# A graph-attention kernel on one core: part-filled gather columns packed densely at computed lane offsets, and more columns weighted by ScalarE in layer 1

## The chip, the core and the metric

The kernel runs on one core of one Trainium2 chip. The metric is the time of one execution on the device in microseconds (us), as a median over runs. Engines go by the profile's names: PE (TensorE, matrix products), DVE (VectorE), ACT (ScalarE), POOL (GpSimd) and SP (SyncE, whose queue issues plain DMAs). Indirect DMAs, which gather rows at addresses that lie in a tile, are issued by GpSimd.

## What is computed

A graph of 6250 nodes with 256 features and 100000 directed edges (`src`, `dst`, sorted by `dst`) goes through three attention layers. Layers 1 and 2 are GATv2 (4 heads of 64) with an ELU between them; their sum with `x` is normalised. Layer 3 is GAT (8 heads of 32) with a residual and a second normalisation. Cut to what matters:

```python
def _gatv2_layer(x, src, dst, n, Wl, Wr, att, b):       # layers 1 and 2, with a loop at each node
    xl = (x @ Wl).reshape(n, H, C)
    xr = (x @ Wr).reshape(n, H, C)
    e = leaky_relu(xl[src] + xr[dst], 0.2)
    logits = einsum('ehc,hc->eh', e, att)
    alpha = softmax of logits over the edges of each dst
    return segment_sum(xl[src] * alpha[:, :, None], dst, n) + b

def _L1_gnn_ref(h, W, a, src, dst):                     # layer 3
    Wh = einsum('nf,hfd->hnd', h, W)
    e = leaky_relu(s1[:, src] + s2[:, dst], 0.2)        # s1, s2: Wh with the halves of a
    attn = softmax of e over the edges of each dst
    out = segment_sum(attn[:, :, None] * Wh[:, src], dst, N)

x = _layernorm(x + _L0_gnn_ref(x, ...))
x = _layernorm(x + _L1_gnn_ref(x, ...))
```

## The kernel before

**Batches and columns.** `make_plan` sorts the nodes by the number of their incoming edges, most first, and cuts them into 49 batches of 128. A batch has one node on each of 128 partitions, called lanes here. Column j of a batch is the j-th neighbour of every lane: one indirect DMA fetches 128 rows of the layer's table (260, 261 or 264 floats each). Since the nodes are sorted, the number of columns falls from batch to batch. The function `columns` fixes the numbers before the run from the expected spread of degrees, 3.5 standard deviations wide: 27 for batch 0, then 25, 24, 23, 22, 21, 21, ... to 10, 10, 9, together 803. A last column of a batch that only a few lanes can fill need not be gathered alone. Ten such columns (of batches 3, 13, 17, 26, 31, 36, 40, 43, 47 and 48) share 3 packs: a pack is one gather of 128 rows whose lanes belong to several batches at fixed offsets, and `lay_rows` (L1415) copies each batch's lanes into its row tile. `lack_rows` (L1422) fills the lanes that are left with a row that belongs to nobody, so that it gets no weight. That makes 796 gathers a layer.

**Row tiles.** The rows of a batch lie in two to four tiles `g` of up to 9 columns, taken in turn from a pool of 9 (`rowp`, ROWS = 9). In layers 1 and 2 column 0 is the node itself.

**Lists.** `near_r` holds for each batch the nodes' own features and the list of neighbours; `start1` (L1887) fetches a batch's part with one indirect DMA, in layer 1 three batches ahead. After a batch in layer 1 the list is overwritten by the neighbours' places in the sorted order (`spots`, L1822), which address the tables of layers 2 and 3.

**Order.** Everything stands in an order written out by hand, and each engine works its own list from front to back. In layers 1 and 2 (`layer2`), iteration b runs `attend(b)`: for each row tile VectorE makes z = max(g, pr), z times `at`, and a sum per head (L1777 for the first tile, made one batch ahead, L1797, L1800, L1801), then the maximum `top` (L1579), and ScalarE the exponentials (L1587). `weighted_sum` multiplies the rows by their weights: VectorE most columns (L1633), ScalarE the last `few` of a batch, one instruction for each column and head (L1629); PE adds the columns up in `acc` (L1640). `few` is a third of the columns in layer 1 and two thirds in layer 2. `finish` turns the sums into the next layer's table rows, which SP writes (L1917 in layer 1, L1960 in layer 2). At the end of the iteration `fetch(b + 2)` lets GpSimd gather the columns of batch b + 2 (`gather_rows`, L1438). Layer 3 goes the same way with a smaller logit step (L2010) and its sums on VectorE (L1662, L1674); there GpSimd also writes the results out, one indirect DMA a batch (L2040).

**From layer to layer.** The three batches with the most columns have their lists sorted by address (`sort_sources`), so that the first 14, 12 and 11 columns of batches 0, 1 and 2 (`EARLY`) come from table rows of batches 0 to 44. Their gathers (`begin`, with the list `soon`) stand behind the last gather of the layer before. The other gathers of the next layer stand behind them and read the whole table.

**Packs before.** `pick_rows` (L1402) copies the lanes' addresses into a small tile `pick` by plain DMAs from SBUF to SBUF, from layer 1's lists and, for the later layers, from `spots`.

## Time and profile before

| | |
|---|---|
| median of 3 runs | 3244.62 us (3239.51 to 3245.31) |
| profiled execution | 3236.04 us, span 3234.2 us |
| DVE busy | 2714.0 us, 84% of the span, 2609 instructions |
| POOL busy | 2414.4 us, 75%, 2587 instructions |
| PE busy | 1399.5 us, 43% |
| ACT busy | 1281.5 us, 40% |
| moved by DMA | 397.64 MB, 123 GB/s; GpSimd's queue 336.86 MB, the queue of SP and ACT 57.08 MB |
| plan | to about 99 us |
| layer 1 | 1549 gathers from `xl_d` in layers 1 and 2 together, from 102.9 us |
| layer 2 | first `soon` gather at 1157.97 us |
| layer 3 | first `soon` gather at 2155.40 us, last gather at 3214.76 us |

Every duration comes from one profiled execution. In a group's row the columns are busy time and the mean of one instruction, then the idle time of the engine just before them and what ended most of it; "issue" is time in which the engine waited for nothing that the profile shows. In a timeline row they are the start, the duration, the engine and line, what it writes and reads, and in brackets the idle time before it. The profile shortens names: `xl_d` stands for the tables of layers 1 and 2 alike.

### The profile page before, as it was taken

The numbers are of one execution on the slowest core, as the hardware profiler recorded it, in microseconds if no ns is written. First come the engines' busy times: TensorE is split into PE (matmuls) and PEld (weight loads), VectorE is DVE, ScalarE is ACT, GpSimd is POOL, SyncE is SP. The second block draws the span as 40 slices with busy tenths as digits, with TensorE's granted clock in tenths as the row PEclk, the third lists the DMA queues.
The fourth block names the chain that finished last, engine by engine and source line by source line (L and its number), as shares of the span: only waits on it lengthen the run. The fifth ranks groups of instructions, "written<-read, shape, count | busy, mean of one in ns | idle before, by whom it ended". The sixth has DMA issues, their size and how long they took to land.

```text
span 3234.2 us, 25459 instructions
## 1 busy us (share of the span) xinstructions
PE 1399.5 (43%) x5423; PEld 1123.4 (35%) x5424; DVE 2714.0 (84%) x2609; ACT 1281.5 (40%) x5161; POOL 2414.4 (75%) x2587
## 2 busy tenths in 40 slices
PE   8356657666676854666556566760000000000000
PEld 6245545555565643545444455550000000000000
DVE  8599999898899979999989999984966766766777
ACT  4234444444445535777667777770000000000000
POOL 5677777777777777777777777777777777777776
PEclk9678888778888886787788778885555555555555
DMA  9444444444444454444444444444333333333333
GB/s 262 123 113 125 119 120 122 118 122 124 123 123 126 126 146 116 122 123 129 128 123 127 133 129 134 135 129 113 108 107 109 110 108 107 109 109 110 109 110 93
DMA packets 176463, 397.64 MB, mean 123 GB/s; under 512 B 50923, under 2 KB 93955, under 8 KB 176283
## 3 DMA queue, kind: packets, MB, share of 16 engines
q0 software_dynamic: 120608, 336.86, 38.7%
q1 hardware_dynamic: 53992, 57.08, 5.8%
q10 hardware_dynamic: 1700, 1.97, 0.2%
q8 instruction: 48, 0.79, 0.1%
q14 instruction: 115, 0.94, 0.1%
HBM read 354.60 MB, written 40.42 MB: 122 GB/s over the span
## 4 chain that ended last, share of the span: by engine, by line
POOL 25%; DVE 18%; issue 14%; DMA 5%; PE 3%; ACT 0%; DVEq 0%; POOLq 0%; ACTq 0%
POOL g L1438 24%; DVE z L1800 4%; DVE lg L1801 4%; DMA g<-xl_d,near_r 3%; DVE z L1797 3%; PE acc L1640 3%; DVE z L1777 2%; DVE g L1633 2%; DMA g<-whs_d,near_r 1%; DVE weighted L1662 1%; POOL out L2040 1%; DMA out<-y,node_i 1%; DVE stats L1684 0%; DVE acc_v L1674 0%; DVE at L1600 0%
## 5 line engine op out<-in xcount | busy, mean ns | idle before, releaser
L1438 POOL DMA_INDIRECT g<-xl_d,near_r x1549 | 1465.6, 946 | 472.6 <-issue 417.6
L1640 PE MATMUL acc<-g,ident 128*128 128x256 f32 x3408 | 966.5, 452 | 631.3 <-DVE g L1633 318.4
L1640 PEld LDWEIGHTS acc<-g,ident 128*128 128x128 f32 x3408 | 778.4, 232 | 820.4 <-DVE g L1633 336.3
L1438 POOL DMA_INDIRECT g<-whs_d,near_r x756 | 719.5, 952 | 230.3 <-issue 220.5
L1629 ACT ACTIVATE g<-g,by 128x64 f32<-128x64 f32 x3080 | 744.9, 336 | 28.4 <-DVE by L1596 28.4
L1801 DVE TENSOR_REDUCE lg<-z 128x28 f32<-128x1820 f32 (+4 forms) x234 | 497.3, 2125 | 8.1
L1800 DVE TENSOR_TENSOR z<-z,at 128x1820 f32<-128x1820 f32 (+4 forms) x234 | 496.6, 2122 | 4.7
L1797 DVE TENSOR_TENSOR z<-g,pr 128x1820 f32<-128x1820 f32 (+3 forms) x138 | 299.6, 2171 | 42.9 <-DMA g<-xl_d,near_r 33.7
L1604 ACT ACTIVATE wt<-lg 128x128 f32<-128x128 f32 (+17 forms) x49 | 14.0, 285 | 801.5 <-DVE lg L1603 801.5
L1674 DVE TENSOR_REDUCE acc_v<-weighted 128x256 f32<-128x3584 f32 (+10 forms) x47 | 319.0, 6787 | 1.6
L1633 DVE TENSOR_TENSOR g<-g,at 128x256 f32<-128x256 f32 (+8 forms) x185 | 273.5, 1496 | 3.3
L1587 ACT ACTIVATE at<-lg,top 128x19 f32<-128x19 f32 (+14 forms) x392 | 115.3, 294 | 378.2 <-DVE top L1579 359.5
L1777 DVE TENSOR_TENSOR z<-g,pr 128x2080 f32<-128x2080 f32 (+4 forms) x96 | 197.8, 2061 | 72.3 <-DMA g<-xl_d,near_r 33.3
L2010 DVE TENSOR_TENSOR lg<-g,s_r 128x56 f32<-128x56 f32 (+4 forms) x111 | 22.9, 214 | 255.5 <-DMA g<-whs_d,near_r 234.6
L1662 DVE TENSOR_TENSOR weighted<-g,wt 128x1792 f32<-128x1792 f32 (+4 forms) x111 | 227.0, 2056 | 0.3
L1563 ACT COPY xT<-pt 128x256 f32<-128x256 f32 x147 | 50.2, 374 | 403.4 <-PE pt L1558 403.4
L1568 PE MATMUL pm<-wcat,xT 128*128 128x260 f32 x392 | 94.2, 383 | 1.4 <-ACT xT L1563 1.4
L1568 PEld LDWEIGHTS pm<-wcat,xT 128*128 128x128 f32 x392 | 74.2, 190 | 13.3 <-ACT xT L1563 2.1
L1587 ACT ACTIVATION_READ_ACCUMULATOR at<-lg,top 128x1 f32 x392 | 73.2, 187 | 0.0
L1568 PE MATMUL pm<-wh_cat,xT 128*128 128x272 f32 x196 | 58.6, 422 | 22.6 <-ACT xT L1563 22.6
L2040 POOL DMA_INDIRECT out<-y,node_i x49 | 49.8, 1015 | 22.8 <-issue 14.1
L1688 ACT ACTIVATE sd<-mv,eps 128x1 f32<-128x1 f32 x98 | 29.0, 296 | 91.5 <-DVE mv L1686 91.3
(267 smaller groups left out, 1591.5 us busy)
## 6 DMA issues: line engine op xcount, KB each, us to landing
g<-xl_d,near_r POOLq DMA_INDIRECT x1549, 2.8
g<-whs_d,near_r POOLq DMA_INDIRECT x756, 2.8
whs_d<-row SPq DMA_DIRECT2D x49, 132.0 KB
xl_d<-row SPq DMA_DIRECT2D x49, 130.0 KB
xr_d<-row SPq DMA_DIRECT2D x49, 130.0 KB
two<-xl_d SPq DMA_DIRECT2D x49, 130.0 KB
two<-xr_d SPq DMA_DIRECT2D x49, 130.0 KB
near_d<-x_all SPq DMA_DIRECT2D x7, 896.0 KB
```

The costliest lines, as they stand in the source:

```text
L1438: nc.gpsimd.indirect_dma_start(out=g[:, j + own - s0, :width], out_offset=None, in_=table, in_offset=source(of, b, j),)
L1568: nc.tensor.matmul(pm, xT[:, c, :], w[:, c, :], start=c == 0, stop=c == 1)
L1587: nc.scalar.activation(wt[:, :, h], lg[:, :S, h], AF.Exp, bias=top[:, h : h + 1], accum_out=den[:, h : h + 1],)
L1629: nc.scalar.mul(g4[:, t, h, :], g4[:, t, h, :], by[:, s0 + t - a0, h : h + 1])
L1633: nc.vector.tensor_mul(g4[:, :m], g4[:, :m], wt[:, s0 : s0 + m, :].unsqueeze(3).to_broadcast([P, m, H, F // H]),)
L1640: nc.tensor.matmul(acc, ident, g4[:, t], start=False, stop=s0 + t == S - 1 and not more)
L1662: nc.vector.tensor_mul(prod[:, s0 - base : s1 - base, :].rearrange("p t (h d) -> p t h d", h=H), g[:, :n, :F].rearrange("p t (h d) -> p t ...
L1674: nc.vector.reduce_sum(part, prod[:, : s1 - base, :].rearrange("p s f -> p f s"), axis=AX.X)
L1777: nc.vector.tensor_max(z, rows[0][:, :n, :W2], xr[:, None, :].to_broadcast([P, n, W2]))
L1797: nc.vector.tensor_max(z, g[:, :n, :W2], xr[:, None, :].to_broadcast([P, n, W2]))
L1800: nc.vector.tensor_mul(z, z, at[:, None, :].to_broadcast([P, n, W2]))
L1801: nc.vector.reduce_sum(lg[:, s0:s1, :], z.rearrange("p t (h d) -> p t h d", h=H2), axis=AX.X)
```

## The change

The column number of every batch stays; which of the columns are gathered as a whole and which by packs changes.

- `lanes_of` (new, before the run) lists every column that fewer than 96 lanes are sure to fill: 33 items (batch, column), among them two columns of batches 1, 2 and 47 and three of 48. For each it gives the most lanes that it may have (`top`, 8 to 128) and bounds `lo` and `hi` on the sum of lanes of all items before it. The columns that stay are `base`, 770 in all. The items fill 14 packs.
- `find_lanes` (new, once, ahead of layer 1's first gather) computes on the chip how many lanes each item has, sums them up by a product with ones and a scan, brings the sums within `lo` and `hi`, and stores them as integers in `lane_i`. `late` collects whether a bound was broken; then the general path would run as well. It also makes `shut`, which is added to the logits of lanes that an item lacks.
- `pick_lanes` (new, layer 1) writes the addresses of each item into the DRAM list `pick_d` at the item's offset, which SP loads into a register (`lane`). The writes overlap: each covers `top` lanes, and the next one overwrites what the item does not fill. When all items of a pack are written, its 128 addresses are read back into `picks[0]`.
- `gather_packs` gathers pack q behind the dense columns of batch `upon[q]` (1, 1, 1, 3, 5, 7, 8, 15, 19, 20, 25, 34, 44, 46), `keep_packs` writes it to DRAM (`pack_d`), and `lay_rows` reads each item's lanes from there, at the register's offset, into the row tile. For the later layers the packs' own addresses are taken from layer 1's rows (`picked`).
- In layer 1 the lists of the batches whose items are needed are fetched before a batch's gathers: those of batches 3 to 20 ahead of batch 1's, to 25 at batch 3, and so on.
- `weighted_sum` in layer 1 gives ScalarE two fifths of a batch's columns instead of a third, at most all but one of the last tile's.
- The 7 `spare` gathers of `make_plan` and the ten adjustments of `most` go; `counts` moves to a pool that outlives the plan.

```diff
@@ columns / lanes_of
-    packs, taken = [], set()
...
+    for b in range(1, NB):
+        size = min(P, N - P * b)
+        for c in range(low, cols[b]):
+            if min(size, over[c] - 3.5 * sd[c] - P * b) < 0.75 * P:
+                base[b] = min(base[b], c)
+                items.append((b, c))
+                top.append(max(8, min(P, -(-math.ceil(over[c] + 3.5 * sd[c] - P * b) // 8) * 8)))
...
+    K = -(-hi[-1] // P)
+    need = [min(items[i][0] for i in range(len(items)) if hi[i] + top[i] > P * q) for q in range(K)]
+    last = [max(i for i in range(len(items)) if lo[i] < P * (q + 1)) for q in range(K)]
@@ make_plan
-    for k in range(SPARE):
-        nc.gpsimd.indirect_dma_start(
-            out=spare[:, k, :], out_offset=None, in_=listed,
-            in_offset=bass.IndirectOffsetOnAxis(ap=begin_i[:, k : k + 1], axis=1),
-        )
@@ tile_by_degree
+    upon = [max(1, b - 1) for b in need]
...
+    def find_lanes(zp, ps):
...
+        for b, own in items_of.items():
+            nc.vector.tensor_scalar(
+                has[:, own[0] : own[-1] + 1], numbers[:, base[b] : cols[b]], counts[:, b : b + 1],
+                None, op0=OP.is_lt,
+            )
+        pn = ps.tile([P, len(items)], F32, name="lane_n", tag="tp")
+        nc.tensor.matmul(pn, ones, has, start=True, stop=True)
+        nc.vector.tensor_scalar(shut, has, -1.0, BIG, op0=OP.add, op1=OP.mult)
...
+    def lane(i):
+        _, (v,) = nc.values_load_multi_w_load_instructions(
+            lane_i[:, i : i + 1], engines=[mybir.EngineType.SP], min_val=lo[i], max_val=hi[i],
...
+        return bass.ds(v, top[i])
+    def pick_lanes(lists):
+        while written[0] < len(items) and items[written[0]][0] < lists:
+            i = written[0]
+            b, c = items[i]
+            nc.sync.dma_start(pick_d[lane(i), :], sources[: top[i], b, c : c + 1])
+            for q in range(K):
+                if filled_by[q] == i:
+                    nc.sync.dma_start(picks[0][:, q : q + 1], pick_d[q * P : (q + 1) * P, :])
+            written[0] += 1
-        nc.sync.dma_start(rows[-1][:n, rows_at[b], :width], held_rows[q][r : r + n, :width])
+    def keep_packs(b, k):
+        for q in packs_at.get(b, ()):
+            nc.sync.dma_start(pack_d[k][q * P : (q + 1) * P, :], held_rows[q][:, : wide[k]])
+            if k == 0:
+                nc.sync.dma_start(
+                    picked[:, q : q + 1], pack_d[0][q * P : (q + 1) * P, W2 : W2 + 1]
+                )
+    def lay_rows(b, rows, cut, own, k):
+        for i in items_of.get(b, ()):
+            j = items[i][1] + own
+            g, s0 = next((g, s0) for g, (s0, s1) in zip(rows, cut) if s0 <= j < s1)
+            nc.sync.dma_start(g[: top[i], j - s0, : wide[k]], pack_d[k][lane(i), :])
+    def shut_lanes(b, lg, own, H):
+        if b in items_of:
+            i0, n = items_of[b][0], len(items_of[b])
+            s = lg[:, base[b] + own : cols[b] + own, :]
+            nc.vector.tensor_add(s, s, shut[:, i0 : i0 + n].unsqueeze(2).to_broadcast([P, n, H]))
@@ layer2, gather(b)
+                if i == 0 and b:
+                    lists = max([b + 2] + [items[filled_by[q]][0] for q in range(K) if upon[q] <= b]) + 1
+                    for k in range(min(NB, lists)):
+                        begins(k)
+                    pick_lanes(lists)
+                gather_rows(b, rows, cut, 1, table, of, width, first, base[b])
+                gather_packs(b, pack_tile, picks[i], table, width)
+                lack_rows(b, rows, cut, 1, table, width)
+                if b == 1:
+                    waiting.append(lambda: (keep_packs(b, i), lay_rows(b, rows, cut, 1, i)))
+                else:
+                    lay_rows(b, rows, cut, 1, i)
+                    waiting.append(lambda: keep_packs(b, i))
@@ layer2, attend(b)
-                few = min(S // 3, cut[-1][1] - cut[-1][0] - 1) if i == 0 else (2 * S - 2) // 3
+                shut_lanes(b, lg, 1, H2)
+                few = min(2 * S // 5, cut[-1][1] - cut[-1][0] - 1) if i == 0 else (2 * S - 2) // 3
@@ layer2, before gather(0)
+                find_lanes(zp, pst)
+                pick_lanes(3)
@@ layer 3: gather_packs, keep_packs, lay_rows and shut_lanes in the same places
```

## The prediction

> **What bounds the kernel now.** I read the page's busy shares first, then its costliest groups, then busy time by stage, then the timelines of GpSimd and of SP's queue around the two changes of layer.
>
> ```profile
> span 3234.2 us, 25459 instructions
> PE 1399.5 (43%) x5423; PEld 1123.4 (35%) x5424; DVE 2714.0 (84%) x2609; ACT 1281.5 (40%) x5161; POOL 2414.4 (75%) x2587
> ...
> L1438 POOL DMA_INDIRECT g<-xl_d,near_r x1549 | 1465.6, 946 | 472.6 <-issue 417.6
> ```
>
> VectorE is the busier engine by share (2714 against 2414 us), but the share is no verdict. A gather takes GpSimd 0.95 us, and 0.30 us of "issue" follows each one: 1.25 us from start to start. The timeline keeps that step without a hole from 102.9 to 3214.8 us: 64 or 65 DMAs in each 80 us. 2489 indirect DMAs at 1.25 us are 3111 us of the span of 3234.2. So GpSimd's queue sets the pace now, and one DMA fewer is worth 1.25 us, as long as nothing else comes last. What else could, the stages show (columns: us, then PE, PEld, DVE, ACT, POOL busy):
>
> ```profile
> core 0: us, PE busy (x) PEld busy (x) DVE busy (x) ACT busy (x) POOL busy (x), PEclk, DMA share, GB/s
> ...
> 380.10:900.90 520.80, 342.49 (x1336) 280.39 (x1337) 470.34 (x382) 229.65 (x940) 394.09 (x417) 0.81 0.45 121
> 900.90:1178.50 277.60, 210.75 (x834) 171.13 (x833) 263.87 (x256) 143.84 (x592) 209.85 (x223) 0.88 0.49 130
> ...
> 1496.20:1910.50 414.30, 249.93 (x911) 198.40 (x912) 376.30 (x305) 294.38 (x1212) 313.16 (x333) 0.79 0.46 128
> 1910.50:2170.40 259.90, 178.66 (x632) 139.39 (x631) 249.84 (x238) 202.69 (x835) 196.55 (x209) 0.83 0.48 133
> 2249.50:3205.10 955.60, 0.00 (x0) 0.00 (x0) 688.98 (x731) 63.57 (x184) 724.41 (x760) 0.50 0.39 109
> ```
>
> The bounds are starts of the softmax maximum (L1579), which VectorE does once a batch: rows one and two are layer 1's batches 9 to 31 and 32 to 48, three and four the same of layer 2, the last is layer 3. VectorE leaves about 0.03 us between instructions, so its true waiting is 50.5 - 382 x 0.03 = 39 us in row one, 13.7 - 7.7 = 6 in row two, 38.0 - 9.2 = 29 in row three, 10.1 - 7.1 = 3 in row four, and over a quarter of layer 3. In the last third of layers 1 and 2 VectorE has almost nothing left to give. There a faster GpSimd only runs ahead, until it meets this:
>
> ```profile
> 1156.59 0.95 POOL L1438 DMA_INDIRECT g<-xl_d,near_r  x1 [0.30 <-issue]
> 1157.97 0.94 POOL L1438 DMA_INDIRECT g<-xl_d,soon  x1 [0.43 <-PE acc L1640]
> ...
> 1204.59 0.95 POOL L1438 DMA_INDIRECT g<-xl_d,near_r  x1 [0.30 <-issue]
> ```
>
> ```profile
> 1153.62 0.33 SPq L1917 DMA_DIRECT2D xl_d<-row  x1
> ...
> 1194.19 0.32 SPq L1917 DMA_DIRECT2D xl_d<-row  x1
> ```
>
> The `soon` gathers of the next layer read rows of batches 0 to 44, so the first of them waits for batch 44's table row; the first `near_r` gather needs batch 48's. Batch 44's write is issued at 1153.62. What a write takes to land is seen at the end of layer 2:
>
> ```profile
> 2147.60 0.34 SPq L1960 DMA_DIRECT2D whs_d<-row  x1
> ```
>
> ```profile
> 2150.40 0.95 POOL L1438 DMA_INDIRECT g<-xl_d,near_r  x1 [0.30 <-DMA whs_d<-row]
> ...
> 2155.40 0.94 POOL L1438 DMA_INDIRECT g<-whs_d,soon  x1 [0.30 <-PE acc L1640]
> ```
>
> GpSimd is released by that landing at 2150.1, 2.5 us after issue. So at the first change of layer batch 44's row is there at 1156.1 and is used at 1157.97: slack 1.9 us. At the second it is 2155.40 - 2150.1 = 5.3 us. Batch 48's rows (1194.19 and 2185.84 plus 2.5) have 8 and 13 us.
>
> **The change, part by part.** *Gathers.* Before, a layer has 803 columns, 10 of them in 3 packs: 796 gathers. After, 770 dense columns and 14 packs: 784. 12 fewer in each layer, 15 us of GpSimd a layer, 45 in all. But not evenly. In layer 2, GpSimd is ahead of its old place by 2 gathers at batch 8, 3 at 20, 6 at 31, 10 at 46, 12 at 48. In layer 1 the node lists (`start1`, one DMA a batch) needed to fill the packs are fetched early: 18 before batch 1's gathers instead of 4. So GpSimd's data there are *later*: by 12 DMAs at batch 1, 24 (30 us) at 8, 20 at 20, 11 at 26, 3 at 31, none at 36, and ahead by 4 at 40 and 12 at 48.
>
> *Layer 1.* From batch 8 to 30 VectorE waits for gathers already, so it slips with them: 30 us at batch 8, 25 at 20, 14 at 26, some 4.5 at 31. It catches up because its 39 us of waiting are used up. From 31 on it is bound by itself. The shutting add comes to 13 of these batches; small VectorE adds of this size take 0.17 to 0.20 us (L1594, L1491), so 2.6 us. ScalarE takes one more column in 17 of them, 0.27 us each (L1633: 0.94 us for 3 columns, 1.75 for 6): 4.6 us. Of the 6 us of waiting perhaps 4 can close. 4.5 - 4 - 4.6 + 2.6 = -1.5: VectorE ends layer 1 about 1.5 us sooner, and with it batch 44's row. GpSimd, 15 us ahead, stands still before `soon` and gains 1.5 + 1.9 = 3.4 us.
>
> *ScalarE's share.* 28 more columns in the layer, four scalings at 0.24 us from start to start: 1 us a batch, 27 us in all, on an engine that works 40 of 80 us. PE reaches these columns last: 26 matmul instructions of batch 42 run from 1096.05 to 1104.9 and ScalarE's four columns are done at 1099.07, so a fifth at 1100.0 is hidden. Without that cover it would be 1 us a batch, some 20 us.
>
> *Layer 2.* GpSimd's data are 6 x 1.25 = 7.5 us earlier at batch 31, where VectorE still waits for them. After it: 13 adds, +2.6, and 1 us of waiting to close: VectorE ends 7.5 - 2.6 + 1 = 6 us sooner beyond the 3.4. Batch 44's row then allows 6 + 5.3 = 11.3 of the 15 us.
>
> *Layer 3.* VectorE has a quarter free, no table follows, so all 15 us count. At its end the last batch has 6 gathers instead of 9, 8.8 us, and VectorE needs 10.5 us for batch 47 (3205.1 to 3215.6); but the step was 13.2 us before, and the gain stays 15.
>
> *Round trips on SP.* Each lane goes pack, DRAM, row tile: 14 writes and 33 reads a layer, each read after a register load (0.63 to 0.76 us on SP before) and an issue of about 0.5. Packs are gathered a batch or more before their lanes are needed, except for batch 1: packs land about 196 in layer 1, kept by 199, laid by 205. VectorE's batch 1 then ends some 28 us late instead of 17, which vanishes behind the 30 us at batch 8. In layers 2 and 3 the same chain ends at about 1250 and 2248, and VectorE comes to it at 1252.4 and 2249.5: hidden with 2 us to spare; without that cover 2 to 5 us. Behind these waits on SP stand the writes of table rows and the loads of `two`; a batch's SP work adds up to some 10 to 15 us, and the shortest batch has 12.5 to 14. Batch 44's write has about 7 us of room behind the lays of 47.
>
> *Filling the picks (layer 1).* Each write of lanes waits for the one before, since they overlap. Ten writes (items 4 to 13) and one read stand between batch 3's node list (141 us) and the packs of batch 1, at 160.5 + 23 x 1.25 = 189 us. A step is issue plus landing: no row has a chained write of 4-byte elements. Below: 0.5 + 2.5 = 3.0 us by the table row; above, what the view of the tile `moved` says of its only DMA, the writes of 152-byte runs to `near_d` (L1237):
>
> ```profile
> DMA to landing us min/median/max: 5.1/7.5/9.1
> ```
>
> that is 0.5 + 7.5 = 8.0. GpSimd's wait is 141 + 11 x step - 189: none up to 4.4 us, 40 us at 8.0. I take 3.0, since 512 bytes are nearest to one small transfer, `moved` being 171 KB. The Trainium skill ("DMA: Bandwidth & Descriptors", the section on the anatomy of one DMA) puts about 2 us of fixed cost on a DMA, mostly the receipt of the write and heaviest in HBM, and its quick reference says that pieces under 512 B are read, modified and written. By the first a step would be an estimated 2.5 us, the chain hidden and the sum the same; the second speaks against this change, and only a run can price it.
>
> *The rest at nothing.* `find_lanes` is some 120 small VectorE instructions, about 15 us before batch 0; VectorE idles 27 us there, and batch 1 comes 17 us later anyway; uncovered, 15. The 7 `spare` gathers (10 us) and ten small operations go from GpSimd's plan, where it then waits 15.3 us for VectorE (L1237).
>
> **Sum.** 3.4 + 11.3 + 15 = 29.7 us. Against the profiled execution (3236.0 us, span 3234.2) that is 3206; it was 8.6 us below the median of 3244.6, so the median becomes 3215.
>
> **Rivals.** *All of it* (10%): VectorE's ends move with GpSimd, 45 us, 3200. For it: VectorE waits 29 to 39 us in mid-layer. Against: the 6 and 3 us at the ends. *Layer 3 alone* (10%): VectorE absorbs nothing, its adds and stalls on PE (`pr` came within 2 us of being late in half of layer 1's batches) eat the rest, 15 us, 3230. *The pick chain, slower than before* (15%): GpSimd waits in layer 1's batch 1. Up to batch 30 nothing lies idle that could win it back, so it counts nearly whole. It decides from a step of (48 + 30) / 11 = 7.1 us; at 8.0, 10 us slower, 3255. For it: SP's order and the row of `moved`. Against: its bytes. *The lanes don't fit their bounds* (1%) and the whole general path runs as well, far slower; the bounds are 3.5 deviations wide.
>
> **How the numbers follow.** Forecast 64%: 3215, with step between 3 and 5.5 us (12 us of wait) and VectorE's ends off by 8 us either way: 3206 to 3228. Eight in ten reaches to the full gain and half of the chain's stall: 3200 to 3238. A measurement here can tell about 0.2%, 6.5 us. Faster by more: the forecast, both smaller-gain rivals, less a tenth for a stall near 25 us, 0.78. Within: 0.06. Slower: 0.16.
>
> **What would show it.** Right: GpSimd's group of gathers falls by 12 a layer at 946 ns; a wait of about 12 us at the first `soon` gather after layer 1, about 4 after layer 2, none in layer 3; VectorE some 25 to 30 us late near 380 us and level by 1180. Wrong: GpSimd waiting for picks near 190 us; waits for `pack_d` on VectorE; waits of VectorE for `pr` beyond 7 us.

## The result, and the profile after

The changed kernel takes 3278.26 us (median of 4 runs, 3276.50 to 3281.29) where the kernel before takes 3244.1: ratio 1.0109, 95% interval 1.0091 to 1.0126. It is slower by 34 us, five times what a measurement can tell; the forecast was 29 us faster. The profiled execution took 3276.66 us.

The page's span, busy shares and largest group:

```profile
span 3274.9 us, 26659 instructions
...
PE 1407.0 (43%) x5425; PEld 1126.5 (34%) x5426; DVE 2729.3 (83%) x2817; ACT 1307.8 (40%) x5274; POOL 2375.4 (73%) x2533
...
L1536 POOL DMA_INDIRECT g<-xl_d,near_r x1503 | 1425.9, 949 | 472.8 <-issue 414.7
```

GpSimd has 54 instructions fewer, since the gathers went as planned, and it is busy 39 us less. But its waits (engine and line, what for; us in all, times, longest) have new entries:

```profile
POOL two L1493 <- DMA pick<-pick_d: 39.8, 4, 21.8
...
POOL g L1536 <- DVE g L1731: 12.7, 2, 12.4
...
POOL g L1536 <- DVE few_got L1544: 8.5, 1, 8.5
```

The first are the packs of batch 1, in GpSimd's timeline:

```profile
202.58 0.95 POOL L1536 DMA_INDIRECT g<-xl_d,near_r  x1 [0.30 <-issue]
203.83 0.95 POOL L1493 DMA_INDIRECT two<-xl_d,pick  x1 [0.30 <-issue]
226.57 0.95 POOL L1493 DMA_INDIRECT two<-xl_d,pick  x1 [21.78 <-DMA pick<-pick_d]
238.57 0.94 POOL L1493 DMA_INDIRECT two<-xl_d,pick  x1 [11.06 <-DMA pick<-pick_d]
...
1199.63 0.95 POOL L1536 DMA_INDIRECT g<-xl_d,near_r  x1 [0.30 <-issue]
1212.93 0.94 POOL L1536 DMA_INDIRECT g<-xl_d,soon  x1 [12.36 <-DVE g L1731]
```

Pack 0 finds its picks, packs 1 and 2 wait 33 us for theirs, and nothing else on GpSimd can run meanwhile. What they wait for is SP's chain of writes (start, time from the first issue to the end of the last, number; the last four lines are the first packs on their way to DRAM):

```profile
151.15 32.84 SPq L1479 DMA_DIRECT2D pick_d<-near_r  x5
194.68 0.34 SPq L1482 DMA_DIRECT2D pick<-pick_d  x1
195.53 21.64 SPq L1479 DMA_DIRECT2D pick_d<-near_r  x4
223.87 0.34 SPq L1482 DMA_DIRECT2D pick<-pick_d  x1
224.72 2.85 SPq L1479 DMA_DIRECT2D pick_d<-near_r  x2
235.83 0.34 SPq L1482 DMA_DIRECT2D pick<-pick_d  x1
...
236.71 0.35 SPq L1500 DMA_DIRECT2D pack_d<-two  x1
239.03 0.33 SPq L1502 DMA_DIRECT2D picked<-pack_d  x1
239.40 0.43 SPq L1500 DMA_DIRECT2D pack_d<-two  x1
242.55 0.33 SPq L1502 DMA_DIRECT2D picked<-pack_d  x1
```

The chain begins at 125.96. Its 14 writes and what follows each of them until SP goes on come to 68.7 + 28.3 + 11.1 = 108 us: 7.7 us a step. Single steps of 24 to 40 lanes took 2.5 to 7 us, those of 104 to 128 lanes 7 to 11 us; the longest (9 to 11 us) came while row gathers ran or were still landing beside them, but the last, of 128 lanes with GpSimd standing still, took 8.6 as well. A pack's write, 128 pieces of 1 KB, holds up the read that waits for it by 2.3 and 3.2 us only (236.71 to 239.03, 239.40 to 242.55). The picks' reads back, also in 4-byte pieces, are short: the last is issued at 235.83 and the pack starts at 238.57.

The third entry is the start. The view of the tile `pick_d` says who waited for its first fill (L1423, 1,920 pieces of 4 bytes, issued at 100.91):

```profile
L1423 SPq DMA_DIRECT2D pick_d<-nowhere x1: 410/410/410, 100.9 to 100.9; - x1
...
  DVE few_got L1544: 21.8, 1
```

The first node list, issued at 101.38, landed at 112.5, 11 us later; before it took 3 us (99.00 to 101.93). The first row gather starts at 113.47 instead of 102.9. That the fill is what the list waits for is the profile's inference. The kernel without picks, below, drops the fill and keeps the three broadcasts issued right behind it; there the first list landed 3.3 us after its issue (100.07 to 103.40).

VectorE's stages, between the same batches as those shown of before:

```profile
core 0: us, PE busy (x) PEld busy (x) DVE busy (x) ACT busy (x) POOL busy (x), PEclk, DMA share, GB/s
465.49:962.64 497.15, 345.40 (x1342) 282.75 (x1343) 468.73 (x393) 241.32 (x992) 372.81 (x393) 0.82 0.52 123
962.64:1234.36 271.72, 204.97 (x828) 166.71 (x827) 261.73 (x267) 158.19 (x652) 193.58 (x206) 0.90 0.54 129
```

It reaches the first 85 us later than before and the end of the second 56 later. Its waiting in the first fell from 39 us to 497.15 - 468.73 - 393 x 0.03 = 17, in the second from 6 to 2: it used up what it had, and that gave back 26 of the 85; 3 more came from its shorter work (some 2 us less in each stretch). So the stall at batch 1 counts at the end of the layer. Batch 44's table row (the write at 1210.11, landed by 1212.6 with the 2.5 us of the prediction) comes just ahead of GpSimd's first `soon` gather at 1212.93; by that working it is this row, and not the `DVE g` that the profile names, that releases it:

```profile
1210.11 0.33 SPq L2022 DMA_DIRECT2D xl_d<-row  x1
```

### The profile page after: what moved, and what is told of

Read it like the earlier page. It is cut to its first block, busy times and chain, and to the rows that moved or that the text cites. A ratio compares the mean times of both kernels' runs of the same rounds, so it can differ in the third digit from the quotient of the medians.

```text
span 3274.9 us, 26659 instructions
## 1 busy us (share of the span) xinstructions
PE 1407.0 (43%) x5425; PEld 1126.5 (34%) x5426; DVE 2729.3 (83%) x2817; ACT 1307.8 (40%) x5274; POOL 2375.4 (73%) x2533
## 4 chain that ended last, share of the span: by engine, by line
POOL 24%; DVE 16%; issue 13%; DMA 7%; PE 3%; ACT 0%; DVEq 0%; POOLq 0%; ACTq 0%; SPq 0%
POOL g L1536 23%; DVE z L1904 3%; DVE lg L1905 3%; DMA g<-whs_d,near_r 3%; DMA g<-xl_d,near_r 3%; PE acc L1738 3%; DVE z L1901 2%; DVE z L1881 2%; DVE g L1731 2%; DMA out<-y,node_i 1%; POOL out L2154 1%; DVE weighted L1760 1%; DVE acc_v L1772 0%; DVE stats L1782 0%; DVE at L1698 0%
## 5 line engine op out<-in xcount | busy, mean ns | idle before, releaser
L1536 POOL DMA_INDIRECT g<-xl_d,near_r x1503 | 1425.9, 949 | 472.8 <-issue 414.7
L1536 POOL DMA_INDIRECT g<-whs_d,near_r x733 | 698.2, 953 | 223.4 <-issue 208.5
L1727 ACT ACTIVATE g<-g,by 128x64 f32<-128x64 f32 x3192 | 771.5, 336 | 31.0 <-DVE by L1694 31.0
L1731 DVE TENSOR_TENSOR g<-g,at 128x256 f32<-128x256 f32 (+7 forms) x185 | 266.2, 1456 | 3.3
L1666 PEld LDWEIGHTS pm<-wcat,xT 128*128 128x128 f32 x392 | 75.3, 193 | 13.7 <-ACT xT L1661 2.1
```

Of the source, the lines that this page charges most:

```text
L1536: nc.gpsimd.indirect_dma_start(out=g[:, j + own - s0, :width], out_offset=None, in_=table, in_offset=source(of, b, j),)
L1666: nc.tensor.matmul(pm, xT[:, c, :], w[:, c, :], start=c == 0, stop=c == 1)
L1727: nc.scalar.mul(g4[:, t, h, :], g4[:, t, h, :], by[:, s0 + t - a0, h : h + 1])
L1731: nc.vector.tensor_mul(g4[:, :m], g4[:, :m], wt[:, s0 : s0 + m, :].unsqueeze(3).to_broadcast([P, m, H, F // H]),)
```

## The experiments

The runs named e, f, g and h were made on four chips on which short instructions reached VectorE late: the kernel before took 3,809 to 3,830 us there. The last two, named k, fell on a chip like that of the first pair (before: 3,237.7). So times are told as ratios to the kernel before on the same chip, and stages are compared only within a kind of chip.

How late, VectorE's timeline shows for the short instructions of `find_lanes`, first in the changed kernel of the result, then in the first run with another first fill (e1):

```profile
117.97 1.80 DVE L1441 MEMSET z<- 128x1 f32 x77
```

```profile
119.38 0.17 DVE L1441 MEMSET z<- 128x1 f32 x10 [0.63 <-issue]
120.10 0.06 DVE L1441 MEMSET z<- 128x1 f32 x1 [0.56 <-issue]
...
138.47 0.34 DVE L1444 TENSOR_SCALAR z<-numbers,counts 128x2 f32<-128x2 f32 x2 [1.17 <-issue]
```

77 of them take 1.8 us in a row on the first chip; on the others a few come every 0.7 us or 1.4 us, as soon as the row gathers run. `find_lanes` took 8 us on the first (117.9 to 125.9) and 73 us in this run (118.2 to 191.2).

**The changed kernel on such a chip.** No edit.

> The changed kernel itself, unaltered, as the yardstick beside the three that follow. On a chip on which the kernel before takes about 3,244 us: 3,278, 1.0109 of before. On the chip of the first four runs, where engines waited some 0.7 us for many an instruction and the kernel before took 3,809 us, it should lie at 3,940 or a little above, as the kernels with a better first fill (3,942) and with the old share (3,940) did.

3942.53 us, ratio 1.0342 (1.0318 to 1.0366): 128 us more than before. The loss is nearly four times that of the first chip and sits in layer 1 again: from the first list to the first `soon` gather its trace has 1404 us, against 1318 in the trace of the kernel before that follows. (The two come from two chips; the changed one is 36 us faster than the median above and the other 25 us slower than its own.)

> The kernel before, unaltered, for its trace beside those of the experiments: on the chips of the first eight runs its time was 3,809 and 3,815. Theory (on these chips short instructions reach an engine at 0.7 us and more apart, which hurts the changed kernel's stretch of some 140 short VectorE instructions ahead of batch 0): batch 0's softmax starts near 150 to 165 us here, where it started at 195 to 239 in the changed kernels. Rival (the start is as late here too): 190 or later, and the difference lies behind batch 0.

That trace of before had batch 0's softmax at 161.9 us; the changed kernel has 194.6.

**The first fill alone.**

```diff
-    nc.sync.dma_start(pick_d.rearrange("(k p) c -> p (k c)", p=P), nowhere)
+    nc.sync.dma_start(pick_d.rearrange("(p k) c -> p (k c)", p=P), nowhere)
```

> Only the order of the lanes in the first fill of the pick list changes: each partition writes 15 neighbouring lanes (128 pieces of 60 B instead of 1,920 of 4 B; every value is the same). Theory (small pieces are what costs): the first node list, which landed at 112.5 us of the changed kernel's trace, lands near 103 as before, the first row gather starts near 105 instead of 113.5, and the time falls by the 8.5 us of that wait, to about 3,270. Rival 1 (the three broadcasts into the tails of the pack tables are in the way): the first list still lands near 112 and the time stays at 3,278. Rival 2 (the wait is only moved, since the packs of batch 1 wait for their picks in any case): the start is early but the wait for the picks at batch 1 grows by the same amount, 3,278.

> The first fill of the pick list in 128 pieces of 60 B instead of 1,920 of 4 B, and nothing else. Theory (small pieces): first node list lands near 103 us, the first row gather starts near 105 instead of 113.5, about 3,270 where the changed kernel has 3,278. Rival 1 (the three broadcasts into the pack tables' tails are in the way; in the first look the list's wait was put down to them): no gain at the start, 3,278. Rival 2 (the wait only moves to the packs of batch 1): early start, the same 3,278.

1.0351 (1.0303 to 1.0398) and, beside the changed kernel's 1.0342, 1.0339 (1.0290 to 1.0389). VectorE could start on the first list 6.2 and 6.1 us after its issue. With the old fill it was 13.3 us on the first of the two chips (the run with ScalarE's share at a third, e4) and 8.1 on the second; in the next experiment, whose fill is smaller still, 5.0 and 3.7. So the pieces of the fill do delay it. But the time did not move: GpSimd came earlier to picks that were no earlier. The chain started at 192 us in both, against 187 and 148 with the old fill, since `find_lanes` runs late on these chips.

**Picks of 512 B a lane, chain kept.**

```diff
-    pick_d = dram.tile([K * P + P, 1], I32, name="pick_d")
+    pick_d = dram.tile([K * P + P, P], I32, name="pick_d")
...
-            nc.sync.dma_start(pick_d[lane(i), :], sources[: top[i], b, c : c + 1])
+            nc.sync.dma_start(pick_d[lane(i), :], near[: top[i], b, c : c + P].bitcast(I32))
...
-                    nc.sync.dma_start(picks[0][:, q : q + 1], pick_d[q * P : (q + 1) * P, :])
+                    nc.sync.dma_start(picks[0][:, q : q + 1], pick_d[q * P : (q + 1) * P, :1])
```

> The pick list in device memory gets 512 B a lane instead of 4 B; each of the 33 writes sends 128 neighbouring integers of each list's row (of which only the first is read back), in order and one after the other as before; the first fill covers only the lanes that no write is sure to reach. Theory (pieces of 4 B are what costs): a step of the chain of writes falls from 7 to 11 us for 104 to 128 lanes to about 3 us, the wait of GpSimd for its picks at batch 1 (21.5 + 10.8 us) and the two later ones (2.7 and 3.6) go, as does the 8.5 us at the start: 3,278 - 47 = about 3,231. Rival (the chain itself costs, each write waits for the one before to land, whatever its pieces): steps stay at 7 us and more, only the start is won, about 3,270. Rival 2 (128 times the bytes, 64 KB a write, slow the row gathers beside it): steps short, but the gathers of batches 0 to 2 land later and less than 30 us is won.

> Picks of 512 B a lane, chain kept. On the chip of the first four runs its steps were 1.6 us where those of 4-byte pieces were 6 to 8. Theory (pieces): 47 us less than the changed kernel, 3,231, faster than before by 0.4%. Rival (chain): 3,270. Rival 2 (VectorE sets the end of layer 1 whatever GpSimd does, so that a wait removed at batch 1 comes back at the first gather of the next layer): the wait there grows from 12 us to some 25 and the time is 3,240 to 3,255.

1.0100 (1.0052 to 1.0149) and 1.0057 (1.0021 to 1.0092): about 105 of the 128 us are gone. SP's timeline of the changed kernel, then of this one, over the same writes:

```profile
147.93 56.84 SPq L1479 DMA_DIRECT2D pick_d<-near_r  x8
212.38 0.34 SPq L1482 DMA_DIRECT2D pick<-pick_d  x1
213.24 18.30 SPq L1479 DMA_DIRECT2D pick_d<-near_r  x4
```

```profile
207.05 11.59 SPq L1480 DMA_DIRECT2D pick_d<-near_r  x8
219.89 0.34 SPq L1483 DMA_DIRECT2D pick<-pick_d  x1
220.75 5.19 SPq L1480 DMA_DIRECT2D pick_d<-near_r  x4
```

Eight writes, each waiting for the one before in both: (212.38 - 147.93) / 8 = 8.1 us a step with pieces of 4 bytes, (219.89 - 207.05) / 8 = 1.6 us with 128 times the bytes in pieces of 512. The two did not meet the same traffic, though: row gathers ran beside most of the first and beside none of the second. The first runs of the last two experiments (e1 and e2, on one chip) are closer: their chains start at 192.3 and 192.7, and no row gather is issued from about 200 on in both. There, from the fourth write on, a step takes 6.0 us on average with 4 bytes and 1.5 with 512. Where most of the chain ran beside row gathers (the kernels with `find_lanes` first, further down, on two chips), it was 7.7 and 4.7, leaving out a step that waited for a list. So it is the size of the piece that makes the step, not the chain and not the bytes, and it makes more of it where no gathers run.

In the wide kernel's trace GpSimd still waits 37 us for the picks of batch 1 (47 in the changed kernel's), because its chain starts only at 207, and 7 to 23 us four times later. The two traces lie 47 us apart, the medians 105: batch 1's softmax starts at 271.1 instead of 273.1, batch 31's at 1158.1 instead of 1197.3, batch 48's at 1500.3 instead of 1556.7. So by these traces most of the gain on such a chip comes behind batch 1.

**4-byte pieces, no chain.** Every write has a constant place of its own and needs no register, and the first fill has pieces of 132 B. The packs hold rows of other nodes than the layers need.

```diff
-            nc.sync.dma_start(pick_d[lane(i), :], sources[: top[i], b, c : c + 1])
+            nc.sync.dma_start(pick_d[i * P : i * P + top[i], :], sources[: top[i], b, c : c + 1])
```

> Each of the 33 writes of picks goes to 128 lanes of its own at a constant place, with its 4-byte pieces kept, so none waits for another and none needs a register; a pack's picks are read from the last of its writes. The packs then hold rows of other nodes than the layers need; number and shape of all transfers are kept. The first fill is in 132 B pieces. Theory (either cause of the step): with the chain cut, the picks of batch 1 are there before GpSimd needs them at 204 us, and 21.5 + 10.8 + 6 + 8.5 us go: about 3,231. Rival (the early lists, 18 in front of batch 1 instead of 4, are what delays batch 1): GpSimd still waits or VectorE is late by as much, and the time stays above 3,260.

> 4-byte pieces, but every write to lanes of its own and at a constant place (the packs hold rows of other nodes than the layers need; number and shape of all transfers kept), first fill in 132 B pieces. Theory (pieces): the writes go out one after another without waiting, some 3 us apart, the picks of batch 1 are there by 175, but each still spends its many pieces on the DMA engines beside the gathers: 3,231 to 3,240. Rival (chain): the same. Rival 2 (the load of the small pieces on the DMA engines delays the gathers themselves): gathers of batches 0 to 1 still land 7 us after their issue and not 2.8, and VectorE's wait for batch 1 stays: above 3,250.

1.0087 (1.0049 to 1.0126) and 1.0070 (1.0045 to 1.0094), as good as the wide picks. GpSimd comes to the packs of batch 1 and finds their picks (204.23, 205.48 and 207.04 in the second run's trace, with waits of 0.30, 0.30 and 0.62 us); three later packs still wait 25 to 31 us each. So the loss needs both: slow small pieces, and each waited for by the next. Either cure takes away most of it on these chips.

**The order of two calls.** `find_lanes` ahead of `find_few`, first with the 4-byte picks, then with the wide ones.

```diff
-                find_few(work, pst)
                 find_lanes(zp, pst)
+                find_few(work, pst)
```

> The changed kernel with its 4-byte picks, and only the places found ahead of the short list instead of behind it. Theory (two separate losses: the steps of the chain, and the chain's late start behind VectorE's short instructions): 20 to 40 us of the changed kernel's 128 us over before go, ratio 1.024 to 1.029. Rival (the chain's steps set the wait for the picks wherever it starts, the gathers of the early lists and of batch 0 taking until then in any case): under 10 us, 1.032 to 1.034.

> Picks of 512 B a lane, and the lanes' places found ahead of the short list's nodes instead of behind them (two calls exchanged), so that VectorE runs these short instructions while it waits for the first node list. Theory (they hold up VectorE ahead of batch 0 and the first write of a pick): 20 to 40 us less than with the wide picks alone where the kernel before takes 3,815 (3,800 to 3,818), and some 6 less where it takes 3,244. Rival (batch 1 is set by its chain of lists, picks, packs and lays, which starts with the lists): no change, 3,838.

1.0212 (1.0167 to 1.0256) with the 4-byte picks, against 1.0342; 1.0029 (1.0003 to 1.0056) with the wide ones, against 1.0057. The first gained more than expected. The second gained less, and its interval meets that of the wide picks alone. A chain that starts late is a loss of its own where `find_lanes` is slow; on a chip like the first one, where it took 8 us, the order was not tried alone.

**Without the bounds' instructions, and packing from batch 6 on.** The first leaves out the memsets of `bound` and the clamping (for these inputs the places are the same); the second changes `range(1, NB)` in `lanes_of` to `range(6, NB)`, with and without them.

> As the kernel with wide picks and the places found first (3,834, 1.0029 of before), without the 95 short instructions that set the places' bounds and the five that hold the places to them; for these inputs the places are the same. Theory (short VectorE instructions arrive one in 0.7 us once the row gathers run, and hold up batch 0): a few us less, up to 15 where these instructions meet the gathers: 1.000 to 1.003 of before. Rival (in that kernel they had ended before the gathers began, so nothing is left of them): the same 1.003.

> As the one before, and columns are packed from batch 6 on instead of batch 1: 13 gathers of packs and 789 gathers a layer instead of 14 and 784 (before: 797), no pack before batch 5, lists 0 to 6 as before in front of batch 5. Theory (what is left of the loss is batch 1's chain of five transfers one behind the other and the 18 early lists): the start is as in the kernel before, and 8 gathers a layer, 3 x 8 x 1.25 = 30 us, are won less what VectorE holds back: 3,785 to 3,800 where before takes 3,815; 3,215 to 3,230 where it takes 3,244. Rival (the loss that is left lies in later batches and at the end, where packs and lays add transfers): 3,830 or more.

> As the first of these four, with columns packed from batch 6 on (13 packs, 789 gathers a layer). With the bounds' instructions it took 1.0066 of before, its batch 0 starting at 193 us where the kernel before had 162. Theory (that start was those instructions meeting the gathers): batch 0 starts near 160, 25 to 30 us less, 0.998 to 1.000 of before. Rival (batch 5's wait for a pack that needs lists up to batch 20 costs it): 1.005 or more.

1.0033 (0.9995 to 1.0072), 1.0066 (1.0041 to 1.0091) and 1.0065 (1.0040 to 1.0089). In the last two the rival's number came; the first does not tell theory (up to 1.003) from rival (1.003). In the last, batch 0's softmax was at 164.9 us and batch 2's at 253.2, even ahead of before's 281.2 in its trace on another chip; but batch 10's was at 538.7 against 522.2 and batch 30's at 1139.7 against 1115.6. By these traces packing later moved the loss from batch 1 to the batches behind 5, whose pack needs lists up to batch 20 and their picks.

**ScalarE's share alone.** In the changed kernel back to a third, then in the kernel before raised to two fifths.

```diff
-                few = min(S // 3, cut[-1][1] - cut[-1][0] - 1) if i == 0 else (2 * S - 2) // 3
+                few = min(2 * S // 5, cut[-1][1] - cut[-1][0] - 1) if i == 0 else (2 * S - 2) // 3
```

> The changed kernel with ScalarE's share of layer 1's columns back at one third; all else as changed. Theory (the share is hidden, as predicted, since layer 1 is set by GpSimd's queue in its larger part): VectorE's weighting gets 7.3 us longer in all, of which at most some 3 us lie in the batches after 31 where VectorE is the bound: 3,278 to 3,281. Rival (ScalarE's larger share is itself what costs, ScalarE being late for the copies of sources and rows): the time falls by over 5 us.

> The kernel before with only ScalarE's share of layer 1's columns raised from one third to two fifths. Theory (hidden, as predicted): within 5 us of before; VectorE's weighting falls by 7.3 us in all. Rival (layer 1 is set by VectorE throughout): 5 to 7 us faster. Rival 2 (ScalarE is late for the next batch's copies with it): slower by 5 us or more.

Back to a third: 1.0286 (1.0182 to 1.0390), which does not tell it from the changed kernel. In the kernel before: 0.9975 (0.9955 to 0.9995), 9 us faster than before, nearest the rival that VectorE sets layer 1 throughout; the interval runs from 2 to 17 us. Of the versions that leave nothing out it is the one that beats both kernels, by a quarter of a per cent, on such a chip.

**Twelve gathers less, nothing packed.** The kernel before with the last column of 12 batches filled by SP; their edges are left out.

```diff
+                if j + 1 == cols[b] and b in less:
+                    nc.sync.dma_start(
+                        g[:, j + own - s0, :width],
+                        bass.AP(tensor=table.tensor, offset=table.offset + NP * width,
+                                ap=[[0, P], [1, width]]),
+                    )
+                    continue
```

> The price of twelve gathers with nothing in their place but a copy: the kernel before, with the last column of 12 batches (8 to 45) filled with the row of no node by a transfer of SP instead of a gather, in each layer; these edges are left out. Theory of the prediction (GpSimd's queue is the bound, VectorE takes back a third): 30 us less than before, 0.992. The plain count: 45 us, 0.988. Rival (on these chips the queue is held up by ScalarE, TensorE and late instructions, whose number does not change): 10 to 20 us, 0.995 to 0.997.

0.9887 (0.9835 to 0.9939): some 40 us, nearest the plain count, though the interval holds the 30 us of the theory as well. On such a chip the gain was there to be had.

**The lists alone, and all but the picks,** on a chip like the first one. In the first the kernel before gathers lists as early as the change does; the second is the kernel with wide picks and `find_lanes` first, without a transfer of picks, so its packs hold rows of other nodes.

```diff
+                if i == 0 and b in {1: 21, 3: 26, 5: 31, 7: 36, 8: 40, 15: 43, 19: 45, 20: 47, 25: 48, 34: 49, 44: 49, 46: 49}:
...
+                        begins(k)
```

```diff
-            nc.sync.dma_start(pick_d[lane(i), :], near[: top[i], b, c : c + P].bitcast(I32))
...
+    nc.vector.tensor_copy(picks[0], node_i[:, :K])
```

> The kernel before with nothing of the change but the order of the lists: 21 lists are gathered before batch 1's rows, 26 before batch 3's and so on, as the packs of the changed kernel need them. The prediction had them cost 1.5 us at the end of layer 1, its queue giving the time back later: ratio 1.000 to 1.001. Rival (on the way VectorE loses time at batch 1 that it does not get back, being the bound of most of layer 1): 14 lists x 1.25 = 17 us, 1.004 or more.

> The kernel with wide picks and the places found first, without any transfer of picks: the packs gather rows by other numbers that are there from the start, so they hold rows of other nodes than the layers need; lists, packs, keeps and lays are all there. With the picks it took 1.0029 of before, where twelve gathers less alone gave 0.989. Theory (what is left of the loss is GpSimd waiting for picks that stand in SP's queue behind the table rows of the batches, 67 us in five waits in one trace): 0.990 to 0.997. Rival (lists, keeps and lays take it): 1.000 or more.

The lists cost 1.0015 (1.0005 to 1.0025), 5 us, between the two expectations. Without the picks the kernel takes 3215.00 us (3213.95 to 3216.36), 0.9931 of before (0.9913 to 0.9948). Its GpSimd, at the packs of batch 1 and at the change of layer:

```profile
189.65 0.95 POOL L1535 DMA_INDIRECT g<-xl_d,near_r  x1 [0.30 <-issue]
190.90 0.95 POOL L1492 DMA_INDIRECT two<-xl_d,pick  x1 [0.30 <-issue]
192.15 0.95 POOL L1492 DMA_INDIRECT two<-xl_d,pick  x1 [0.30 <-issue]
193.40 0.95 POOL L1492 DMA_INDIRECT two<-xl_d,pick  x1 [0.30 <-issue]
...
1143.14 0.95 POOL L1535 DMA_INDIRECT g<-xl_d,near_r  x1 [0.30 <-issue]
1158.05 0.95 POOL L1535 DMA_INDIRECT g<-xl_d,soon  x1 [13.96 <-DVE g L1730]
```

The packs go out in step. The trace of the kernel with the lists alone is the slowest of its ten runs, 4 us over their median. The stages by starts of GpSimd's indirect DMAs, in the four traces of this kind of chip, in us:

| stage | before | lists alone | without picks | changed |
|---|---|---|---|---|
| plan, to the first list | 99.0 | 101.3 | 100.1 | 101.4 |
| layer 1, to the first `soon` | 1059.0 | 1067.2 | 1058.0 | 1111.6 |
| layer 2, to layer 3's first `soon` | 997.4 | 998.0 | 985.7 | 987.0 |
| layer 3, to its last gather | 1059.4 | 1059.4 | 1042.3 | 1045.5 |
| from there to the end | 19.4 | 19.5 | 28.5 | 29.5 |
| span | 3234.2 | 3245.3 | 3214.6 | 3274.9 |

## Why the prediction was wrong

**Where the loss is.** Between the kernel without picks and the changed one lie 60 us, 54 of them in layer 1. Of these GpSimd's waits for picks at batch 1 are 32 (21.8 + 11.1, less the usual 0.3 each), the later first gather 8 (12.1 us after the first list's issue against 4.3), two more pack waits 6, at batches 20 and 34. That the transfers of picks cost the change its gain is shown by taking them away (with them went the first fill, and `find_lanes` was put first); that it is their 4-byte pieces in a row, by the runs with wide picks and without a chain, on the slower chips, and on the first chip by the packs' writes of 1 KB pieces beside it (2.3 and 3.2 us a step). What the wide picks take on a chip like the first was not run.

**The step that failed: "I take 3.0".** The step of the chain was put between 3.0 us, from a table row's landing, and 8.0, from `moved`, and the lower was taken because 512 bytes are few. It is 7.7. But the row chosen is hardly nearer in bytes (a table row's write is 128 runs of about 1 KB, some 130 KB, `moved` 171 KB), and in pieces it is the farther one: `moved` has runs of 152 bytes, the chain has 4. Put into the prediction's own formula, 141 + 11 x 7.7 - 189 = 37 us, and GpSimd waited 33. That they come so close is in part luck, as both ends of the formula moved by some 15 us: the chain's first four writes, which it passes over, held the fifth until 156.24, and GpSimd came to pack 1 at 204.8. The Trainium skill's rule that pieces under 512 B are read, modified and written ("DMA: Bandwidth & Descriptors", Specifications), which was set beside it as speaking against the change, is the side on which the runs came down: 1.5 us a step with 512 B and 6.0 with 4 B, on one chip with GpSimd standing still. No run shows the reading and modifying itself. By the same page's fixed cost of some 2 us, which it gives in its section on DMAs that GpSimd issues while these are SP's, the chain would have been hidden.

**The rival had it.** "The pick chain, slower than before" had a chance of 15%, a point of decision of 7.1 us and 3255 us at 8.0. The direction, the place and the step are right, and the sign that the prediction named came, GpSimd waiting for picks, at 205 us instead of 190. The other 23 us, and 7 more because the wait was 33 and not 40, are what neither case had: the first fill, which "the rest at nothing" passed over (8 us at the first gather); the plan, longer by 2.4 us (by 2.3 with the lists alone, where there is no fill); the two later pack waits (6); gathers of 949 instead of 946 ns and 1.2556 instead of 1.2525 us from start to start (2,440 of them, 7.5); and the end (10). These come to 34, so a few are given back elsewhere.

**The rest of the sum held.** Without picks, layer 1 gave 1.0 us (forecast 3.4), layer 2 11.7 (11.3), layer 3 to its last gather 17.1 (15). GpSimd stood still for 13.7 us at the first `soon` gather without picks and 12.1 in the changed kernel (12 forecast), and for 3.2 and 2.9 after layer 2 (4 forecast). So VectorE takes back nearly all of GpSimd's 15 us in layer 1 and a fifth in layer 2, as the stages of before said. Without picks it is 34 us late at 380 us (413.7) and 2 at 1180, where the forecast had 25 to 30 and level. Two counts were off by little: behind batch 31 ScalarE took one more column in 15 batches, not 17 (652 instructions for 592, four a column), and there are 11 shutting adds, not 13 (267 for 256). The predicted 3215 is what the kernel without picks takes, though for a smaller gain from its own before: 22.7 us instead of 29.7. The end, next, cost it 9.

**The end was mis-sized.** "The gain stays 15": from the last gather to the end it is 29.5 us instead of 19.4. VectorE's additions of node scores in the changed kernel, then the last of them in the kernel before:

```profile
3237.22 0.20 DVE L2123 TENSOR_TENSOR lg<-g,s_r 128x40 f32<-128x40 f32 x1
3240.37 0.25 DVE L2123 TENSOR_TENSOR lg<-g,s_r 128x40 f32<-128x40 f32 x1 [2.95 <-DMA g<-whs_d,near_r]
...
3252.37 0.23 DVE L2123 TENSOR_TENSOR lg<-g,s_r 128x72 f32<-128x72 f32 x1 [0.41 <-issue]
```

```profile
3218.28 0.23 DVE L2010 TENSOR_TENSOR lg<-g,s_r 128x72 f32<-128x72 f32 x1 [1.89 <-DMA g<-whs_d,near_r]
```

Batch 48's last gather is issued at 3245.40 and lands at 3248.4, but VectorE comes to it at 3252.37, 12.0 us after batch 47's second tile. That is 7.0 us after the issue; before it was 3.5 (3214.76 to 3218.28). With 6 gathers in the last batch VectorE's own work on a batch is longer than GpSimd's, so 3.5 us of what is saved there are not gained.

Most of the rest lies behind the last output. From its issue to the end of the span it is 12.3 us instead of 6.0:

```profile
3262.56 0.98 POOL L2154 DMA_INDIRECT out<-y,node_i  x1 [8.60 <-DVE y L2196]
```

```profile
3228.20 0.99 POOL L2040 DMA_INDIRECT out<-y,node_i  x1 [8.37 <-DVE y L2082]
```

There GpSimd's queue closes with two instructions that the busy time does not count, `INC_SWDGE_SEM` (1.7 us instead of 0.5) and `DRAIN` (ns, shortest, median and longest of three; first changed, then before):

```profile
L2226 POOLq DRAIN  x3: 50/107/6275, 3267.8 to 3274.6; - x3
```

```profile
L2112 POOLq DRAIN  x3: 46/107/1137, 3232.2 to 3233.9; - x3
```

The two take 1.6 us in all four traces with 2,513 indirect DMAs (the plan's included), 8.0 in all thirteen with 2,470, 8.7 in the one with 2,477 and 9.5 in the two with 2,485, on either kind of chip. They go with that number in every trace here; no run shows why. The kernel without picks pays these 6.4 us too; without them its 22.7 would be 29.

**Lists and share.** Alone the early lists cost 5 us. The prediction had VectorE level again at the end of layer 1 in spite of them, but together with gathers saved, and so it is without picks (2 us late at batch 48). In the kernel with the lists alone VectorE is 21 us late at batch 1, 16 at 30 and 12 at 48 (2 of these from its plan), and GpSimd waits 8.8 us at the first `soon` gather. The share was not only hidden: alone it brought 9 us (2 to 17) on a chip of the slower kind, where the forecast counted 4.6 us in layer 1's batches from 31 on.

## What to carry to other kernels

Where a step's cost is bounded by two rows, take the row that is like it in what costs: for a transfer to device memory the number and size of its pieces, not its bytes, and for a chain multiply the wrong choice by its length before choosing. A gather saved from a queue that bounds the kernel is worth its step, but the list that says where to gather must not be made on that queue's path: give its elements full pieces or places of their own and, which no run here tried, have them ready a batch ahead. Count the last batches by themselves: what is saved behind the point where another engine's work on a batch is longer is not gained, and what the queue does after its last transfer belongs to the time as well.

## What the runs showed that was not expected

- Up to 64 KB in pieces of 512 B went in steps of 1.5 us, up to 512 bytes in pieces of 4 B in steps of 6.0, on the same chip with no row gathers beside them. What ran beside the small pieces was slow too: row gathers issued while the chain ran landed 7.8 us after issue (median, 126 to 236 us), against 2.8 over the same time in the kernel without picks.
- How long GpSimd's queue takes to close went with the number of its indirect DMAs in every trace: 1.6 us with 2,513, 8.0 with 2,470, 9.5 with 2,485.
- On four of the five chips used later short instructions came to VectorE 0.7 us apart while gathers ran, and the kernel before took 17 to 18% longer. A stretch of a hundred short instructions is 8 us on one chip and up to 73 on another.
- Gathers were 3 ns slower in the changed kernel than in the one before and the one without picks. No run settled why.
